# Folding the softmax totals across partitions by adding transfers, so that TensorE sums three tiles instead of eight for the denominators

## The chip, the core and the metric

The kernel runs on one core of a Trainium2 chip. The metric is the device time of one execution in microseconds (us); lower is better. The core has five engines with instruction queues of their own: TensorE (PE in the profile, with its weight loads as PEld), VectorE (DVE), ScalarE (ACT), GpSimd (POOL) and SyncE (SP). Each works through its queue in order and waits on semaphores for what other engines and transfers (DMAs) produce.

## The reference, cut to what matters

Two layers run one after the other on an image tensor of shape 2 x 256 x 64 x 64. The change lies in the first layer, an attention over all 4096 pixels of an image with 8 heads of 32 channels:

```python
q = proj(Wq, bq) / math.sqrt(hd)
k = proj(Wk, bk)
v = proj(Wv, bv)
attn = jax.nn.softmax(jnp.einsum('bnd,bmd->bnm', q, k), axis=-1)
fuse = jnp.einsum('bnm,bmd->bnd', attn, v)
fuse = fuse.transpose(0, 2, 1).reshape(B, C, H, W)
hybrid = _conv1x1(jnp.concatenate([x, fuse], axis=1), Wf, bf)
return hybrid * m + x * (1.0 - m)
```

The second layer computes a channel gate, an attention in 8 x 8 windows, and two 7 x 7 grouped convolutions that give a sigmoid gate. Everything is float32.

The softmax divides by the sum of the exponentials over the 4096 keys. The kernel multiplies the unnormalised exponentials with v, sums the exponentials beside that, and divides afterwards.

## The kernel before, in words

**Work order.** After the projections, `pipeline` (L523) goes through 1024 slots, a list of (b, c, g, m): image b (2), chunk c of 512 queries (8), group g of four heads (2), block m of 128 keys (32). A chunk is therefore 64 slots. This text numbers the 16 chunks 0 to 15 in order of time, and the slots from the chunk's first one, so that slot 63 is a chunk's last and slots 64 on lie in the next chunk. The order on every engine is the order in which the loop at L1196 issues the instructions (`tc.manual_schedule`): in slot i the scores of slot i+2 (L633, TensorE), their exponentials (L646, ScalarE, into a ring of 8 buffers `e`), the products of slot i with v (L669, TensorE), and the sum of the exponentials of slot i (L675, VectorE).

**The totals.** VectorE adds the tiles `e` (128 keys x 4 heads x 512 queries) into two running totals `sum` and `odd`, one for even and one for odd slots ("two chains"), and at a group's last slot adds the two (L677). What remains is a tile of 128 partitions x 4 heads x 512 queries, whose 128 partitions are still to be summed. The last chunk has only one chain, since the buffer of the second is then taken by the convolution.

**The denominators.** `denominators()` (L690) sums the partitions on TensorE: for each of the 8 heads four matmuls (one for each 128 queries, each into its own 32 output partitions) with the constant weights `keysum`, which hold ones in the column of that head. The 32 matmuls add into one PSUM tile `dn`, of which ScalarE makes the copy `inv` (L702); VectorE takes the reciprocal (L721); GpSimd's queue stores it to DRAM (L707, four transfers) and reads it back spread over 32 partitions for each head into `rd` (L714, four transfers); VectorE multiplies the attention result `f` with it (L727).

**Delays written out by hand.** `at(delay, action)` puts an action off by so many slots; `run_later` issues what is due at the end of a slot. The denominators come DN = 8 slots after a chunk's last slot, thus in slot 71; reciprocal, store and spread in slot 72; the multiplication L727 in slot 78. In slot 79 the chunk is handed to `stage` (L731), a generator that does the rest of the chunk in steps; `run_stages` takes a step in every fourth slot, the first in slot 80. The first step multiplies x and f with WfT (`hy`, L519): 32 instructions with x, then 32 with f. The last step adds into `xo` (L974) and stores it to `xs` (L989, GpSimd's queue). For chunk 0, L727 comes 9 slots and the first step 12 slots later.

**Buffers.** Tiles with one `tag` share the buffers of that tag. `psum2` has two PSUM buffers in this phase; `dn` takes one of them between two scores. The totals `sum` have three buffers.

Of the kernel before, what the change touches and what calls it, by code (L numbers as in the profile page):

```python
# [10 lines left out]
F32 = mybir.dt.float32  # L11
I32 = mybir.dt.int32
AF = mybir.ActivationFunctionType
ALU = mybir.AluOpType
# [3 lines left out]
B, C, H, W = 2, 256, 64, 64  # L18
N = H * W
P = 128  # L20
KC = C // P
CH = 512
NCHUNK = N // CH
HEADS0, HD0 = 8, 32
NPAIR = HEADS0 // 2
HG = 4
# [4 lines left out]
EB = 8  # L31
DN = 8
# [16 lines left out]
UW = UG * KS  # L49
# [8 lines left out]
def conv_seq_kernel(ctx: ExitStack, tc: tile.TileContext, a, out):  # L58
    nc = tc.nc
    const = ctx.enter_context(tc.tile_pool(name="const", bufs=1))  # L60
# [12 lines left out]
    def psum2(name):  # L73
        return ps["pair"].tile([P, 2, CH], F32, tag="s", name=name)
# [19 lines left out]
    keysum = const.tile([P, HEADS0, 4, HEADS0], F32, name="keysum")  # L94
    nc.gpsimd.memset(keysum, 0.0)
    for h in range(HEADS0):
        nc.gpsimd.memset(keysum[:, h, :, h : h + 1], 1.0)
    xo = const.tile([P, KC, WS, WP], F32, name="xo")
    nc.gpsimd.memset(xo, 0.0)
    cbias1 = const.tile([P, NU], F32, name="cbias1")  # L100
# [226 lines left out]
    def spread(row, n):  # L327
        f = row.shape[-1]
        return row.rearrange("p u f -> u p f").to_broadcast([NU, n, f])
# [37 lines left out]
    with (  # L367
# [8 lines left out]
        for n in ("WqT", "WkT", "WvT"):  # L376
            t = w0.tile([P, KC, C], F32, name=n)
# [4 lines left out]
        for n in ("bq", "bk"):  # L382

            t = w0.tile([P, KC], F32, name=n)
# [31 lines left out]
        for i, (b, c) in enumerate(chunks):  # L416
            load_chunk()
            x = xs0[i]
            sq = st0.tile([P, 2 * KC, CH], F32, tag="sq", name=f"sq_{b}_{c}")
            tops = st0.tile([P, 2 * KC, CH // 4], F32, tag="top4", name=f"top4_{b}_{c}")  # L420
            for n, w in (("q", wq), ("k", wk)):
                s = psum2(f"{n}0_{b}_{c}")
                for g in range(KC):
                    for kc in range(KC):
                        rhs = x[:, kc, :]
                        if n == "q":
# [5 lines left out]
                            start=(kc == 0),  # L432
                            stop=(kc == KC - 1),
                        )
                t = st0.tile([P, KC, CH], F32, tag=n, name=f"{n}st_{b}_{c}")
# [24 lines left out]
        for i, (b, c) in enumerate(chunks):  # L460
            s = psum2(f"v0_{b}_{c}")
            sv = s.rearrange("p a (t o) -> p (a t) o", t=2)
            for m in range(4):
                for kc in range(KC):
# [4 lines left out]
                        start=(kc == 0),  # L469
                        stop=(kc == KC - 1),  # L470
# [21 lines left out]
            elif i == 2:  # L492
# [3 lines left out]
                for oc in range(KC):  # L496
                    for kc in range(KC):
# [4 lines left out]
                            start=(kc == 0),  # L502
                            stop=(kc == KC - 1),
# [19 lines left out]
    def pipeline(arm, shifted, pools):  # L523
        fp, xpool, gp, wp, avp, ctx_conv = pools
        cpool = ctx_conv.enter_context(tc.tile_pool(name=f"conv{arm}", bufs=1))
# [14 lines left out]
            for g in range(KC)  # L540
            for m in range(NMB)
        ]
        kts, vts, qts, xts, fts, mts = {}, {}, {}, {}, {}, {}
        es, acc, first, totals = {}, {}, {}, {}
        now = [0]
        later = deque()
        stages = deque()

        def at(delay, action):
            later.append((now[0] + delay, action))  # L550
# [13 lines left out]
        def load_q(b, c):  # L564
            q = qp.tile([P, KC, CH], F32, tag="q", name=f"q{arm}_{b}_{c}")
            nc.sync.dma_start(q, q_s[b, c].rearrange("p (g n) -> p g n", g=KC))
            qts[b, c] = q
# [83 lines left out]
            return lambda: exp(*parts[-1])  # L651


        def products(i):
            b, c, g, m = slots[i]
            chains = 1 if (b, c) == (B - 1, NCHUNK - 1) else 2
            if m == 0:
                acc[0] = avp.tile([P, CH], F32, tag="av", name=f"av{arm}_{i}")
                acc[1] = ep.tile([P, HG, CH], F32, tag="sum", name=f"sum{arm}_{i}", bufs=3)
                totals[b, c, g] = acc[1]  # L660
                if chains == 2:
                    room = cpool.tile([P, ROOM], F32, tag="room", name=f"odd{arm}_{i}")
                    acc[2] = room[:, 0 : HG * CH].rearrange("p (h n) -> p h n", h=HG)
            av = acc[0]
            e, v = es[i], vts[b, c, g, m // PB]
            start, stop = m == 0, m == NMB - 1
            for j in range(HG):
                r = slice(32 * j, 32 * j + 32)
                nc.tensor.matmul(av[r, :], v[:, m % PB, r], e[:, j, :], start=start, stop=stop)  # L669
            e = es.pop(i)  # L670
            if m < chains:
                first[m] = e
            else:
                total = acc[1 + m % chains]
                nc.vector.tensor_add(total, first.pop(m % chains, total), e)  # L675
            if stop and chains == 2:
                nc.vector.tensor_add(acc[1], acc[1], acc[2])  # L677
            if stop:
                if g == 0:
                    fts[b, c] = fp.tile([P, KC, CH], F32, tag="f", name=f"f{arm}_{b}_{c}")  # L680
                f = fts[b, c]
                nc.scalar.copy(f[:, g, :], av)
                if g == 0:
                    return
                both = [totals.pop((b, c, gg)) for gg in range(KC)]
                inv = fp.tile([P, P], F32, tag="inv", name=f"inv{arm}_{i}")
                rd = fp.tile([P, KC, 4, P], F32, tag="rd", name=f"rd{arm}_{i}")


                def denominators():  # L690
                    s = psum2(f"dn{arm}_{i}")
                    for h in range(HEADS0):
                        for q in range(4):
                            r = slice(32 * q, 32 * q + 32)
                            nc.tensor.matmul(  # L695
                                s[r, 0, 0:P],
                                keysum[:, h].rearrange("p i h -> p (i h)"),
                                both[h // HG][:, h % HG, q * P : (q + 1) * P],
                                start=(h == 0),
                                stop=(h == HEADS0 - 1),  # L700
                            )
                    nc.scalar.copy(inv, s[:, 0, 0:P])  # L702


                def store_inv(engines):
                    for q in range(4):
                        engines[q % len(engines)].dma_start(  # L707
                            inv_s[b, c][:, :, q].rearrange("h g n -> g h n"),
                            inv[32 * q : 32 * q + HEADS0],
                        )  # L710

                def spread(engines):
                    for h in range(HG):
                        engines[h % len(engines)].dma_start(  # L714
                            rd[32 * h : 32 * h + 32].rearrange("p g q n -> p (g q n)"),
                            inv_s[b, c][h].rearrange("g q n -> (g q n)").partition_broadcast(32),
                        )

                late = EB + 1 if (b, c) == (0, 0) else 0
                at(DN, denominators)  # L720
                at(DN + 1, lambda: nc.vector.reciprocal(inv, inv))  # L721
                queues = (nc.gpsimd,)
                if (b, c) == (B - 1, NCHUNK - 1):
                    queues = (nc.sync, nc.gpsimd)
                at(DN + 1, lambda: store_inv(queues))
                at(DN + 1, lambda: spread(queues))
                at(DN + 7 + late, lambda: nc.vector.tensor_mul(f, f, rd.rearrange("p g q n -> p g (q n)")))  # L727

# [271 lines left out]
        def convolve():  # L1002
# [8 lines left out]
            for k in range(2):  # L1011
                t = cpool.tile([P, B * nb, WP], F32, name=f"yc{arm}{k}")
# [4 lines left out]
            weights = deque([*range(1, NU), 1])  # L1017
            dst = out.rearrange("b (g i) r w -> b i r g w", i=4)

            def load_w(u):  # L1020
                if u >= NU:
                    return
                n = 2 * 32 * UW
                if u == 0:
                    t = cpool.tile([P, n], F32, name=f"w{arm}{u}")
                else:
                    t = ep.tile([P, HG, CH], F32, tag="e", name=f"w{arm}{u}")
                    t = t.rearrange("p h n -> p (h n)")[:, 0:n]
                nc.sync.dma_start(t, w_s[u])
                ws[u] = t  # L1030
# [149 lines left out]
        def run_stages():  # L1180
            while stages:
                waits = next(stages[0], stages)
                if waits is not stages:
                    return waits
                stages.popleft()
# [9 lines left out]
            scores(i)()  # L1195
        for i, (b, c, g, m) in enumerate(slots):  # L1196
            now[0] = i
            if (b, c, g, m) == (B - 1, NCHUNK - 1, 0, 12):
                for _ in banded:
                    pass  # L1200
                conv = convolve()
                next(conv)
            if m % PB == 0:
                load_piece(i // PB + AHEAD)
            if g == KC - 1 and m == 0:
                nxt = (b, c + 1) if c + 1 < NCHUNK else (b + 1, 0)
                if nxt[0] < B:
                    load_q(*nxt)
            rest = scores(i + 2) if i + 2 < len(slots) else None
            products(i)  # L1210
            if rest:
                rest()
            if g == KC - 1 and m == NMB - 1:
                late = EB + 5 if (b, c) == (0, 0) else 0
                at(DN + 8 + late, lambda b=b, c=c: stages.append(stage(b, c)))
            run_later()
            if i % 5 == 1:
                next(banded, None)
            if i % 4 == 0:
                run_stages()  # L1220
# [102 lines left out]
```

## Time and profile before

| | us |
|---|---|
| median of 3 runs | 2924.72 (2922.76 to 2928.86) |
| the profiled execution, its own time | 2921.04 |
| its span in the profile | 2919.3 |
| PE busy | 2881.9 (99%) |
| ACT busy | 2455.9 (84%) |
| DVE busy | 2434.9 (83%) |
| POOL busy | 315.1 (11%) |
| denominators on PE (L695) | 1% of the chain that ended last |
| granted TensorE clock, mean | 0.996 |

The span is the stretch from the first to the last instruction of the profiled execution. "Busy" is the time in which an engine worked on an instruction. Matmuls overlap one another and their ends are modelled, so a busy PE isn't PE at its peak, and the distance between the starts of two groups tells more than their durations. The timeline of an engine gives on each line the start, the duration, the engine, the line of the code, the operation, the tiles written and read, the shapes and how many instructions were merged; in brackets the engine's idle time ahead and what ended it.

### The profile page before, as it was taken

To read this page: it belongs to the slowest core of one execution; us is meant where nothing else is said; L and a number is where in the kernel's file an instruction comes from. 1 tells how busy PE (TensorE), PEld (TensorE's weight loads), DVE (VectorE), ACT (ScalarE), POOL (GpSimd) and SP (SyncE) were. 2 spreads that over 40 slices of the span, in tenths; PEclk is the share of its full clock that TensorE was granted. 3 is DMA by queue.
4 is the path that set the end of the run, shared out by engine and by line. 5 is a ranking of instruction groups with operands and counts; after the bars stand their busy time and mean duration, and the time that the engine had idled before them with its cause. 6 is when DMAs were issued, how large, how long until landed. Compare 5 with 4: busy or idle time off the path is not lost.

```text
span 2919.3 us, 85528 instructions
## 1 busy us (share of the span) xinstructions
PE 2881.9 (99%) x37322; PEld 837.2 (29%) x37322; DVE 2434.9 (83%) x1356; ACT 2455.9 (84%) x4143; POOL 315.1 (11%) x560
## 2 busy tenths in 40 slices
PE   9999999999999999999999999999999999999998
PEld 3551222222222222222222222222222222222665
DVE  3339999899999898998989999989899899999211
ACT  5569989898989898988989898989899898989433
POOL 8010000000000101010000000000101010000356
PEclk9999999999999999999999999999999999999999
DMA  8545422222232323242222223222324232232474
GB/s 245 202 172 174 134 75 63 78 68 80 56 88 65 90 61 91 65 80 71 70 75 69 79 55 82 64 83 63 77 73 84 70 73 75 69 113 88 117 228 120
DMA packets 231124, 276.26 MB, mean 95 GB/s; under 512 B 118672, under 2 KB 135252, under 8 KB 230484
## 3 DMA queue, kind: packets, MB, share of 16 engines
q1 hardware_dynamic: 200996, 231.74, 27.3%
q0 software_dynamic: 22416, 35.61, 5.5%
q8 instruction: 295, 4.83, 0.7%
q10 hardware_dynamic: 7328, 3.36, 0.4%
q14 instruction: 89, 0.73, 0.1%
HBM read 221.88 MB, written 66.39 MB: 99 GB/s over the span
## 4 chain that ended last, share of the span: by engine, by line
PE 97%; DMA 1%; ACT 1%; DVE 0%; issue 0%; SPq 0%; POOL 0%; ACTq 0%; DVEq 0%; POOLq 0%
PE sa L633 37%; PE ava L669 35%; PE hya L519 4%; PE qka L519 4%; PE c2a L1082 2%; PE q L428 2%; PE c1a L1057 2%; PE opa L519 2%; PE vwa L519 2%; PE v L465 2%; PE k L428 2%; PE dna L695 1%; PE sca L847 1%; PE pta L922 1%; PE oa L941 1%; PE ca2a L785 1%
## 5 line engine op out<-in xcount | busy, mean ns | idle before, releaser
L646 ACT ACTIVATE ea<-sa 128x512 f32<-128x512 f32 (+1 forms) x3072 | 2036.7, 746 | 51.6 <-PE sa L633 26.6
L633 PE MATMUL sa<-qa,ka 32*64 32x512 f32 x16384 | 1145.9, 613 | 1.5 <-ACT vst L473 1.2
L675 DVE TENSOR_TENSOR suma<-suma,ea 128x2048 f32<-128x2048 f32 x480 | 1097.4, 2286 | 5.7 <-ACT ea L646 0.5
L669 PE MATMUL ava<-ea,va 128*32 128x512 f32 x8192 | 1091.1, 605 | 1.0
L675 DVE TENSOR_TENSOR odda<-odda,ea 128x2048 f32<-128x2048 f32 x420 | 959.4, 2284 | 50.6 <-ACT ea L646 50.6
L633 PEld LDWEIGHTS sa<-qa,ka 32*64 32x64 f32 x16384 | 241.7, 129 | 785.4 <-ACT ea L646 713.6
L669 PEld LDWEIGHTS ava<-ea,va 128*32 128x32 f32 x8192 | 161.5, 108 | 834.1 <-issue 804.6
L989 POOL DMA_DIRECT2D xs<-xo x94 | 66.6, 716 | 1761.8 <-DVE xo L974 1758.8
L675 DVE TENSOR_TENSOR suma<-ea,ea 128x2048 f32<-128x2048 f32 x32 | 73.2, 2287 | 58.8 <-ACT ea L646 58.8
L519 PE MATMUL qka<-ua,qkv_w 128*32 128x512 f32 x1024 | 115.8, 592 | 0.3 <-DVE ua L803 0.3
L1130 POOL DMA_DIRECT2D out_dram<-za x180 | 101.3, 571 | 77.8 <-DVE za L1110 56.3
L447 DVE TENSOR_REDUCE top<-sq 128x512 f32<-128x2048 f32 x16 | 36.6, 2286 | 81.6 <-ACT sq L441 81.6
L750 ACT ACTIVATE ta<-hya,bf 128x512 f32<-128x512 f32 x32 | 20.2, 683 | 97.3 <-PE hya L519 91.3
L1110 DVE TENSOR_TENSOR za<-za,xla 128x768 f32<-128x768 f32 x24 | 23.0, 960 | 94.3 <-ACT za L1099 53.7
L707 POOL DMA_DIRECT2D invs<-inva x62 | 34.1, 558 | 599.2 <-DVE inva L721 438.9
L754 DVE TENSOR_TENSOR ta<-ta,mca 128x512 f32<-128x512 f32 x32 | 22.0, 688 | 77.4 <-ACT ta L750 77.4
L868 ACT ACTIVATE ewa<-ewa,mxwa 128x64 f32<-128x64 f32 x256 | 85.3, 346 | 1.5 <-DVE mxwa L859 1.5
L1082 PE MATMUL c2a<-yca,wa 32*64 32x192 f32 (+1 forms) x2688 | 83.7, 387 | 2.6 <-issue 2.3
L1093 ACT ACTIVATE za<-c2a 128x384 f32<-128x384 f32 x64 | 27.8, 486 | 57.9 <-PE c2a L1082 41.6
L826 ACT ACTIVATE qka<-qka,qkv_b 128x512 f32<-128x512 f32 x64 | 40.3, 681 | 40.8 <-PE qka L519 40.8
L1082 PEld LDWEIGHTS c2a<-yca,wa 32*64 32x64 f32 x2688 | 64.7, 192 | 22.0 <-issue 12.7
L677 DVE TENSOR_TENSOR suma<-suma,odda 128x2048 f32<-128x2048 f32 x30 | 68.8, 2292 | 1.0
(138 smaller groups left out, 1675.9 us busy)
## 6 DMA issues: line engine op xcount, KB each, us to landing
ka<-ks SPq DMA_DIRECT2D x256, 256.0 KB
va<-vs SPq DMA_DIRECT2D x256, 256.0 KB
wa<-ws SPq DMA_DIRECT2D x17, 896.0 KB
ws<-zeros SPq DMA_DIRECT2D x16, 896.0 KB
xs<-xo POOLq DMA_DIRECT2D x78, 140.0 KB, 6.0
xla<-xs SPq DMA_DIRECT2D x24, 420.0 KB
x<-in_x_dram SPq DMA_DIRECT2D x16, 512.0 KB
qs<-qst SPq DMA_DIRECT2D x16, 512.0 KB
```

What stands on the lines that cost most here:

```text
L428: nc.tensor.matmul(s[:, g, :], w[:, kc, g * P : (g + 1) * P], rhs, start=(kc == 0), stop=(kc == KC - 1),)
L465: nc.tensor.matmul(sv[:, m, :], xs0[i][:, kc, m * P : (m + 1) * P], wv[:, kc, :], start=(kc == 0), stop=(kc == KC - 1),)
L519: nc.tensor.matmul(out[o : o + 32], weights[:, o : o + 32], x, start=start, stop=stop)
L633: nc.tensor.matmul(heads[j][o], k[r, cols][:, o], q[r, g, :], start=True, stop=not shifted)
L646: nc.scalar.activation(e[:, h, :], tile, AF.Exp, scale=SCALE0)
L669: nc.tensor.matmul(av[r, :], v[:, m % PB, r], e[:, j, :], start=start, stop=stop)
L675: nc.vector.tensor_add(total, first.pop(m % chains, total), e)
L677: nc.vector.tensor_add(acc[1], acc[1], acc[2])
L868: nc.scalar.activation(e[:, n, :], e[:, n, :], AF.Exp, bias=mx[:, n : n + 1], accum_out=rs[:, n : n + 1],)
L989: eng.dma_start(x_s[b, n, p + r0 : p + r1].rearrange("r g w -> g r w"), xo[64 * h : 64 * h + 64, oc, r0 - WS * c : r1 - WS * c, :],)
L1082: nc.tensor.matmul(tiles[j // 2][o, j % 2, 0 : n * W], w[r, d, o], y[r, 0:n, d : d + W], start=(d == 0), stop=(d == KS - 1),)
L1130: eng.dma_start(*args)
```

## The change

`fold` is new. When the total of group 0 of a chunk is done (slot 31), 16 transfers on GpSimd's queue lay its four quarters of 32 partitions on top of one another: for each head, the first quarter is copied, and the other three are added by the transfer itself (`accum_op=add`). The four heads come to lie in the four quarters of one tile of 128 partitions x 512. For group 1 (slot 63) it is eight transfers: each head is folded once, to 64 partitions, and two heads share a tile. The results are three tiles of 128 x 512, which lie in one buffer with the tag `w0`; a tile of the convolution's weights, which had a buffer of its own, now shares it. `denominators` has three steps of four matmuls with the new constant weights `foldsum`, instead of eight steps with `keysum`.

The denominators move from slot 71 to slot 73, reciprocal, store and spread from 72 to 74, L727 from 78 to 80 (chunk 0: 87 to 89). The hand-over to `stage` moves from slot 79 to 80, and since L727 stands ahead of it in the list, the first step still falls in slot 80, now right behind L727 (chunk 0: slot 92, as before). The last chunk keeps its old way. In the last chunk the generator of the convolution, with its first loads, is created in slot 16 instead of slot 12.

```diff
@@ constants
+    foldsum = const.tile([P, 3, 4, HEADS0], F32, name="foldsum")
+    nc.gpsimd.memset(foldsum, 0.0)
+    for h in range(HEADS0):
+        n, rows = (0, 32) if h < HG else (1 + (h - HG) // 2, 64)
+        p = rows * (h % HG if h < HG else h % 2)
+        nc.gpsimd.memset(foldsum[p : p + rows, n, :, h : h + 1], 1.0)
+    foldsum = foldsum.rearrange("p n i h -> p n (i h)")
@@ pipeline
+        def fold(total, b, c, g):
+            if g == 0:
+                t = cpool.tile([P, 2 * 32 * UW], F32, tag="w0", name=f"fold{arm}_{b}_{c}")
+                folds[b, c] = [t[:, n * CH : (n + 1) * CH] for n in range(3)]
+            rows = 32 * (g + 1)
+            for k in range(P // rows):
+                for h in range(HG):
+                    dst = folds[b, c][0 if g == 0 else 1 + h // 2]
+                    p = rows * (h if g == 0 else h % 2)
+                    nc.gpsimd.dma_start(
+                        dst[p : p + rows],
+                        total[rows * k : rows * k + rows, h, :],
+                        accum_op=ALU.add if k else ALU.bypass,
+                    )
@@ products
                 nc.scalar.copy(f[:, g, :], av)
+                if chains == 2:
+                    fold(totals.pop((b, c, g)), b, c, g)
                 if g == 0:
                     return
-                both = [totals.pop((b, c, gg)) for gg in range(KC)]
+                both = [] if chains == 2 else [totals.pop((b, c, gg)) for gg in range(KC)]
+                parts = folds.pop((b, c), [])
@@ denominators
-                    for h in range(HEADS0):
+                    terms = [
+                        (keysum[:, h].rearrange("p i h -> p (i h)"), both[h // HG][:, h % HG, :])
+                        for h in range(HEADS0 if both else 0)
+                    ]
+                    terms += [(foldsum[:, n], part) for n, part in enumerate(parts)]
+                    for n, (weights, x) in enumerate(terms):
                         for q in range(4):
                             r = slice(32 * q, 32 * q + 32)
                             nc.tensor.matmul(
                                 s[r, 0, 0:P],
-                                keysum[:, h].rearrange("p i h -> p (i h)"),
-                                both[h // HG][:, h % HG, q * P : (q + 1) * P],
-                                start=(h == 0),
-                                stop=(h == HEADS0 - 1),
+                                weights,
+                                x[:, q * P : (q + 1) * P],
+                                start=(n == 0),
+                                stop=(n == len(terms) - 1),
                             )
@@ delays
-                at(DN, denominators)
-                at(DN + 1, lambda: nc.vector.reciprocal(inv, inv))
+                wait = DN + 2 * (chains == 2)
+                at(wait, denominators)
+                at(wait + 1, lambda: nc.vector.reciprocal(inv, inv))
...
-                at(DN + 1, lambda: store_inv(queues))
-                at(DN + 1, lambda: spread(queues))
-                at(DN + 7 + late, lambda: nc.vector.tensor_mul(f, f, rd.rearrange("p g q n -> p g (q n)")))
+                at(wait + 1, lambda: store_inv(queues))
+                at(wait + 1, lambda: spread(queues))
+                at(wait + 7 + late, lambda: nc.vector.tensor_mul(f, f, rd.rearrange("p g q n -> p g (q n)")))
@@ load_w
-                    t = cpool.tile([P, n], F32, name=f"w{arm}{u}")
+                    t = cpool.tile([P, n], F32, tag="w0", name=f"w{arm}{u}")
@@ loop over slots
-            if (b, c, g, m) == (B - 1, NCHUNK - 1, 0, 12):
+            if (b, c, g, m) == (B - 1, NCHUNK - 1, 0, 16):
...
-                late = EB + 5 if (b, c) == (0, 0) else 0
-                at(DN + 8 + late, lambda b=b, c=c: stages.append(stage(b, c)))
+                late = EB + 4 if (b, c) == (0, 0) else 0
+                at(DN + 8 + ((b, c) != (B - 1, NCHUNK - 1)) + late, lambda b=b, c=c: stages.append(stage(b, c)))
```

## The prediction, made before the changed kernel ran

> **What bounds the kernel now.** I read the busy times first, then the chain that ended last, then the waits, then timelines of chunk 3, which stands for chunks 2 to 13.
>
> ```profile
> PE 2881.9 (99%) x37322; PEld 837.2 (29%) x37322; DVE 2434.9 (83%) x1356; ACT 2455.9 (84%) x4143; POOL 315.1 (11%) x560
> PE 97%; DMA 1%; ACT 1%; DVE 0%; issue 0%; SPq 0%; POOL 0%; ACTq 0%; DVEq 0%; POOLq 0%
> ACT inva L702 <- PE dna L695: 13.4, 16, 1.3
> ```
>
> TensorE is the bound, 97% of the chain, and around the denominators ScalarE waits for it: 13.4 us for all 16. So TensorE time taken out there should leave the span. The timeline of TensorE around them gives the price (start, duration, line):
>
> ```profile
> 810.61 1.07 PE L669 MATMUL ava<-ea,va 128*32 128x512 f32 x8
> 811.61 1.11 PE L633 MATMUL sa<-qa,ka 32*64 32x512 f32 x16
> 812.65 1.07 PE L669 MATMUL ava<-ea,va 128*32 128x512 f32 x8
> 813.53 1.93 PE L695 MATMUL dna<-suma,keysum 128*32 128x128 f32 x64
> 815.39 1.11 PE L633 MATMUL sa<-qa,ka 32*64 32x512 f32 x16
> ...
> 833.64 3.62 PE L519 MATMUL hya<-xa,WfT 128*32 128x512 f32 x32
> 837.08 3.62 PE L519 MATMUL hya<-fa,WfT 128*32 128x512 f32 x32
> ```
>
> A slot lasts 2.04 us (score to score, 809.57 to 811.61). The products take 1.00 us to the next start where scores follow (810.61 to 811.61), but 0.88 where the denominators follow (812.65 to 813.53): the difference, 0.12 us, is the change from arrays of 128*32 to 32*64. The denominators take 815.39 - 813.53 = 1.86 us, less that 0.12 leaves 1.74, or 0.218 us for each of eight heads.
>
> VectorE is next. Its timeline of the same chunk (L677 is slot 63, L721 slot 72, L727 slot 78):
>
> ```profile
> 796.80 2.29 DVE L677 TENSOR_TENSOR suma<-suma,odda 128x2048 f32<-128x2048 f32 x1
> ...
> 816.17 0.95 DVE L721 RECIPROCAL inva<-inva 128x128 f32<-128x128 f32 x1
> ...
> 830.18 1.22 DVE L727 TENSOR_TENSOR fa<-fa,rda 128x1024 f32<-128x1024 f32 x1
> 831.32 2.29 DVE L675 TENSOR_TENSOR odda<-odda,ea 128x2048 f32<-128x2048 f32 x1
> 833.52 2.29 DVE L675 TENSOR_TENSOR suma<-suma,ea 128x2048 f32<-128x2048 f32 x1
> ```
>
> An add takes 2.20 us (831.32 to 833.52), more than a slot. Between stage steps VectorE falls behind, without a gap from slot 66 to slot 80, and catches up while TensorE does `hy` (it then waits 5.70 us for ScalarE, L754). f is ready at 831.40 and wanted at 837.08: 5.68 us to spare.
>
> **The Trainium skill.** "TensorE: Matmul & The Clock Gate", Part 3, says that matmuls start and end strictly in order: a denominator that waits for a transfer holds all scores and products behind it. The trace agrees in chunk 15, where `hy` waits 1.7 us for L727 and nothing overtakes. "TensorEngine Tiling (Array Packing)", Key Properties, says that a change of tiling mode drains the array: here 0.12 us. "DMA: Bandwidth & Descriptors", Rules for kernel authors, says that an adding transfer must wait for the earlier one into the same bytes; that makes the rounds below. Its fit (Anatomy of one DMA), 2.0 us + bytes/436e3, would be 2.15 to 2.3 us for 64 to 128 KB; the trace has 3.2 us for 128 KB, and I use that. None of these prices an adding transfer.
>
> **The change part by part.**
>
> *Matmuls.* Five of eight groups go in 15 chunks: 5 x 0.218 = 1.09 us a chunk, 15 x 1.09 = 16.4 us. The drain stays. ScalarE doesn't take the gain's place: it idles about 0.8 us on each side of L702 there and needs 0.27 us for it. The waits for transfers ahead of these matmuls cost TensorE's sequencer from 0 to 0.2 us a chunk (one such wait on L695 shows 0.05 us, and there may be four); the queue runs ahead, I take 0.
>
> *Transfers.* 24 a chunk, 360 in all, 31 MB, on POOL's queue. An issue takes 0.5 to 0.7 us (L707 0.56, L989 0.72), so about 200 us of an engine that is 11% busy. For an adding transfer the landing is bounded by 1.6 us (the shortest L707) and 10.8 us (the longest L989), since no trace shows one. I take 3.2, the row that moves as much:
>
> ```profile
> rda<-invs POOLq DMA_DIRECT2D x62, 128.0 KB, 3.2
> xs<-xo POOLq DMA_DIRECT2D x78, 140.0 KB, 6.0
> ```
>
> Group 0's four rounds start at slot 31, when POOL has nothing else, and have 40 slots. Group 1 has two rounds: 0.3 us to start, landing of the first round 3.2, 0.2 for the semaphore, three more issues 1.65, landing 3.2: 8.6 us. They start at the end of L677, 799.09. The denominators come at 813.53 + 2 x 2.04 = 817.6, 18.5 us later. Cover: ten slots; it is gone at a landing of 8.2 us. Behind the waiting transfers in POOL's queue stand the eight stores L989 (799.99 before, now about 806, 5.8 us); nobody waits for them before the next chunk. Then come L707 and L714, which would be held only if L989 landed after 822.
>
> *Chunk 0* is tighter: VectorE lags by four slots, L677 ends at 330.80, and slot 73 is 337.39 + 4.08 = 341.5. That is 10.7 us for 8.6, enough up to a landing of 4.2.
>
> *The move by two slots.* L721, L707, L714 and L727 keep their distances of six slots, but two adds now stand ahead of L727: it ends 2 x 2.20 = 4.40 us later, while TensorE is 1.09 us earlier. To spare in chunks 2 to 13: 5.68 - 4.40 - 1.09 = **0.19 us**. The cover of L727 is used up. The spread now matters too: in the trace it landed 0.3 to 3.1 us ahead of L727, and in chunk 6 L727 waited 0.64 us, which would now cost 0.45. Two slots change what the transfers meet, so I take 0.2 us a chunk (0 to 0.6). Chunk 1, where VectorE runs level with TensorE, has 5.08 - 4.40 = 0.7 to spare. Chunk 0: 4.22 - 4.40 - 1.09 = -1.27, so its gain is lost and 0.2 us with it.
>
> *Chunk 14* is different, since the next chunk has one chain of adds, 2.39 us each, and one add more:
>
> ```profile
> 2580.84 1.22 DVE L727 TENSOR_TENSOR fa<-fa,rda 128x1024 f32<-128x1024 f32 x1
> 2583.76 3.62 PE L519 MATMUL hya<-fa,WfT 128*32 128x512 f32 x32
> ```
>
> L727 ends at 2582.06 + 4.77 = 2586.8; TensorE would want it at 2583.76 - 1.09 = 2582.7. It waits 4.1 us, net +3.0. VectorE, which waited 1.5 us at L754 here, now waits about 4.4; it has some 1 us of gaps left in the last chunk, so this isn't won back.
>
> *The rest.* Nine memsets (about 1 us) at the start stand on POOL ahead of loads of small weights, while TensorE projects for 185 us; cost 0, at most 1 if that cover fails. The shared buffer `w0` is wanted by the next fold at slot 95, 22 slots after the denominators; the convolution's loads come four slots later but are used 44 slots on. Both 0, at most 1 us if SP's queue waited for the buffer with key loads behind it.
>
> Sum: chunks 1 to 13, 13 x (-1.09 + 0.2) = -11.6; chunk 0 +0.2; chunk 14 +3.0: **-8.4 us**. The profiled execution's own time is 2921.04 (span 2919.3 and 1.7 around it): 2912.6. It stands 3.7 below the median of the runs, 2924.72: **2916** there.
>
> **The rivals.**
>
> *The spread or VectorE eats the gain (no change).* Every delay of f over 0.19 us is paid by TensorE at once. For: landings of L714 vary from 2.5 to 6.0 us, and POOL and the transfers get more to do. Against: the folds are over before L707. If f came 0.9 us late on average in 13 chunks, -14.2 + 11.7 + 3.2 = +0.7: 2925.
>
> *The folds become the bound (slower).* The place: the first matmul of the denominators, slot 73. The price: what two rounds take above 18.5 us, so it begins at a landing of 8.2 us and passes the gain at 8.8. For: an adding transfer must read its destination too, and L989, strided, reaches 10.8. Against: rows of 2 KB, 64 to 128 KB. At 9 us, two rounds take 20.2: 1.7 late, net 0.6 x 13 = 8; chunk 0 late by 9.5, net 8.4; chunk 14 3: +19, 2944. At 10 us about 2970.
>
> *The heads are not independent.* If each transfer waited for the one before, group 1 would need 8 x 3.4 = 27 us, 8.7 late: 13 x 7.6 and some 20 in chunks 0 and 14, about 2920 + 119 = 3043. Against: the four L714, into four quarters of `rd`, are issued 0.5 us apart.
>
> **How the numbers follow.** A measurement can tell about 0.2%, 5.8 us, from no change. Forecast 0.62, from 2909 (no late f, none in chunk 14 either) to 2921 (0.6 us in each chunk); of it 0.55 lie below 2918.9 and 0.07 within. Gain eaten, 0.16: 0.14 within, 0.02 slower. Late folds 0.18 and serial folds 0.04, slower. Faster 0.55, same 0.21, slower 0.24. The range goes from 2909 to 2940, which leaves out the serial folds and most late folds.
>
> **What would show it.** Right: L695 with 24 instructions in 0.77 us to the next score, no wait on it; L727 directly ahead of `hy` with f, TensorE waiting under 0.5 us for it in most chunks and about 4 in chunk 14; chunks of 157.7 to 158 us instead of 158.8. Wrong: a wait of L695 for a transfer (landings over 8 us), or a wait of `hy` for L727 of a microsecond in every chunk.

## The result and the profile after

| | before | after |
|---|---|---|
| median of 14 runs each, in turn on one chip, us | 2925.09 (2921.39 to 2930.67) | 2925.60 (2919.37 to 2929.27) |
| profiled execution, own time (span), us | 2921.04 (2919.3) | 2927.96 (2926.2) |
| start of the last convolutions (first matmul L1088, before L1057), us | 2700.25 | 2696.27 |
| from there to the end of the span, us | 219.01 | 229.91 |

The ratio is 0.9998 [0.9991, 1.0005]: no change, against a forecast of 8.4 us less. The two profiled executions make it look like a loss, since that of before lies 4.1 us under its median and that of after 2.4 us over its own. The two last rows show the pattern all the same: a gain up to the end of the slots, and a larger loss in the 8% of the span that follow, where the change touches almost nothing. (I call these two stretches **the slots** and **the rest**.)

The page of after, busy times and chain:

```profile
PE 2873.4 (98%) x36722; PEld 821.6 (28%) x36722; DVE 2437.0 (83%) x1356; ACT 2455.0 (84%) x4143; POOL 568.6 (19%) x929
PE 91%; DMA 3%; DVE 2%; issue 2%; ACT 1%; POOL 1%; SPq 0%; ACTq 0%; DVEq 0%; POOLq 0%
```

TensorE has 600 matmuls and 8.5 us of work less (the trace counts two for each of these matmuls of the code, of which 300 are gone), yet its share of the chain fell from 97% to 91%: it now waits. For what, its table of waits says (total, times, longest, us; "issue" is time in which it waited for nothing that the profile shows):

```profile
PE hya L526 <- DVE fa L758: 9.1, 5, 4.0
PE c1a L1088 <- ACT yca L1096: 6.3, 2, 5.7
PE c1a L1088 <- issue: 5.9, 2, 4.5
...
PE dna L725 <- DMA folda<-suma: 3.0, 2, 1.9
```

Before, `hy` waited once for f, 1.7 us; "issue" ahead of the convolutions cost 2.3 us, on L1082. L526, L725, L758 are the former L519, L695, L727.

**The gain is there.** TensorE's timeline in chunk 3:

```profile
817.29 0.84 PE L725 MATMUL dna<-folda,foldsum 128*32 128x128 f32 x24
818.06 1.16 PE L640 MATMUL sa<-qa,ka 32*64 32x512 f32 x16
...
832.27 3.62 PE L526 MATMUL hya<-xa,WfT 128*32 128x512 f32 x32
836.80 3.64 PE L526 MATMUL hya<-fa,WfT 128*32 128x512 f32 x32 [0.91 <-DVE fa L758]
```

The denominators take 818.06 - 817.29 = 0.77 us instead of 1.86, in each of chunks 1 to 14 and without a wait. But f comes late here: `hy` with f starts 4.53 us after `hy` with x, where it took 3.44 before: 1.09 us, the whole gain of this chunk. The chain of waits in this stretch shows who made f late (start, duration, what):

```profile
799.05 3.55 DMA folda<-suma
...
805.35 1.64 POOL folda L670 x2
806.99 0.65 POOL xs L1020
...
807.87 8.83 DMA xs<-xo
...
823.14 6.19 DMA invs<-inva
...
831.39 4.00 DMA rda<-invs
...
835.52 1.24 DVE fa L758
```

The folds hold GpSimd's queue until 807. So the eight stores to `xs` (L1020, before L989) are issued from 806.4 to 814.9, instead of 800.0 to 806.8, and the last lands at 827.4. The inverse's stores were issued at 821.5 to 823.7, into that traffic, and the last takes 6.19 us. The spread can't be issued before 829.9 and lands at 835.4; VectorE is ready 1.2 us earlier. The page prices the transfers (busy us, mean ns of one issue; then KB and median us to landing):

```profile
L670 POOL DMA_DIRECT2D folda<-suma x360 | 252.7, 899 | 1787.7 <-DVE suma L699 1043.2
...
folda<-suma POOLq DMA_DIRECT2D x240, 64.0 KB, 3.1
folda<-suma POOLq DMA_DIRECT2D x120, 128.0 KB, 3.9
...
xs<-xo POOLq DMA_DIRECT2D x78, 140.0 KB, 7.9
```

In the slots of the profile of after, the last `xs` store landed after the inverse's first store was issued in chunks 3, 6 and 12 (by 5.9, 1.1 and 0.7 us), and in no other from 2 to 14, as far as landings are recorded. These are the three whose f was late by the spread: 1.09, 1.15 and 0.69 us. In the other ten of chunks 1 to 13, f was ready 0.22 us (chunk 1: 0.53) ahead of `hy`. The stores to `xs` aren't the whole reason, though. In a second profile of after, chunks 4, 5 and 13 also had such a landing, by 1.0 to 1.9 us, without a late f. And in the kernel before, these same three chunks have the longest time from the inverse's first store to the first issue of the spread: 6.1, 5.9 and 6.5 us in its second profile, against 4.7 to 5.0 in the other nine of chunks 2 to 13 (in its first, 5.1 to 5.5 against 4.6 to 5.2). There f has about 5 us or more to spare, so it costs nothing. What makes these three slow wasn't tested.

**Chunk 0** waits for its folds:

```profile
340.75 0.40 PE L725 MATMUL dna<-folda,foldsum 128*32 128x128 f32 x8
342.28 0.43 PE L725 MATMUL dna<-folda,foldsum 128*32 128x128 f32 x8 [1.13 <-DMA folda<-suma]
344.62 0.43 PE L725 MATMUL dna<-folda,foldsum 128*32 128x128 f32 x8 [1.91 <-DMA folda<-suma]
344.97 1.11 PE L640 MATMUL sa<-qa,ka 32*64 32x512 f32 x16
```

4.22 us to the next score instead of 0.77. The first transfer of group 1's first round was issued at 330.38 and landed at 337.03; the second round landed at 344.48.

**Chunk 14** waits for VectorE, and then runs at half clock:

```profile
2570.40 3.62 PE L526 MATMUL hya<-xa,WfT 128*32 128x512 f32 x32
2578.07 5.34 PE L526 MATMUL hya<-fa,WfT 128*32 128x512 f32 x32 [4.05 <-DVE fa L758]
2583.33 1.11 PE L640 MATMUL sa<-qa,ka 32*64 32x512 f32 x16
```

The second line should last 3.62 us. The table by stretches, whose column behind the five busy times (PE, PEld, DVE, ACT, POOL) is PEclk, the granted clock, says why:

```profile
2578.10:2579.10 1.00, 1.00 (x12) 0.38 (x16) 0.00 (x0) 0.00 (x0) 0.00 (x0) 0.99 0.00 0
2579.10:2582.50 3.40, 3.40 (x24) 0.85 (x16) 0.00 (x0) 0.00 (x0) 0.00 (x0) 0.50 0.02 5
2582.50:2585.90 3.40, 3.40 (x48) 0.62 (x40) 1.62 (x3) 2.43 (x4) 0.00 (x0) 1.00 0.00 0
```

The wait cost 4.23 us, the half clock 1.7 more.

**The rest.** It is 10.90 us longer, and four places make up about that much. L526 waits for f of chunk 15 2.63 us instead of 1.68 (+0.97 between its two halves), and the half clock after that wait makes it 5.34 us long (+1.72). The stretch from the 13th to the 15th group of c1a takes 19.10 us instead of 12.43 (+6.67). And the span goes on for 15.89 us behind TensorE's last matmul, instead of 14.25 (+1.64). The wait ahead of the ninth group of c1a is longer too, 5.73 us instead of 4.09, but adds nothing: counted from the start of the rest, the group comes 2.57 us later, no more than the wait for f and its half clock. TensorE's timeline, chunk 15 and then the stretch:

```profile
2709.05 3.63 PE L526 MATMUL hya<-xa,WfT 128*32 128x512 f32 x32
2715.30 5.34 PE L526 MATMUL hya<-fa,WfT 128*32 128x512 f32 x32 [2.63 <-DVE fa L758]
...
2801.52 2.20 PE L1088 MATMUL c1a<-xla,wa 128*32 128x192 f32 x47
2805.10 0.70 PE L1088 MATMUL c1a<-xla,wa 128*32 128x192 f32 x9 [1.37 <-issue]
2805.73 2.64 PE L1113 MATMUL c2a<-yca,wa 32*64 32x192 f32 x112
2808.30 0.56 PE L1088 MATMUL c1a<-xla,wa 128*32 128x192 f32 x6
2813.34 4.64 PE L1088 MATMUL c1a<-xla,wa 128*32 128x192 f32 x50 [4.49 <-issue]
```

Before, the same groups go through:

```profile
2802.48 2.54 PE L1057 MATMUL c1a<-xla,wa 128*32 128x192 f32 x56
2804.95 2.64 PE L1082 MATMUL c2a<-yca,wa 32*64 32x192 f32 x112
2807.52 2.54 PE L1057 MATMUL c1a<-xla,wa 128*32 128x192 f32 x56
```

In after, TensorE stands still in the middle of a group, without a semaphore to wait for. The two places are 127 matmuls with their weight loads apart, 254 instructions. The group behind the longer standstill takes 4.64 us at half clock instead of some 2.3.

So the questions were: is the loss in the rest the change's doing or chance; what are chunks 0, 3, 6, 12 and 14 worth; and what is the standstill?

### The profile page after: what moved, and what is told of

Same layout as the page of the kernel before. It is cut to its first block, busy times and chain, and to the rows that moved or that the text cites. A ratio compares the mean times of both kernels' runs of the same rounds, so it can differ in the third digit from the quotient of the medians.

```text
span 2926.2 us, 84951 instructions
## 1 busy us (share of the span) xinstructions
PE 2873.4 (98%) x36722; PEld 821.6 (28%) x36722; DVE 2437.0 (83%) x1356; ACT 2455.0 (84%) x4143; POOL 568.6 (19%) x929
## 4 chain that ended last, share of the span: by engine, by line
PE 91%; DMA 3%; DVE 2%; issue 2%; ACT 1%; POOL 1%; SPq 0%; ACTq 0%; DVEq 0%; POOLq 0%
PE sa L640 34%; PE ava L691 33%; PE qka L526 4%; PE hya L526 3%; PE c1a L1088 2%; PE c2a L1113 2%; PE vwa L526 2%; PE opa L526 2%; PE v L472 2%; PE q L435 2%; PE k L435 1%; DVE suma L697 1%; DMA invs<-inva 1%; PE sca L878 1%; PE oa L972 1%
## 5 line engine op out<-in xcount | busy, mean ns | idle before, releaser
L670 POOL DMA_DIRECT2D folda<-suma x360 | 252.7, 899 | 1787.7 <-DVE suma L699 1043.2
L526 PE MATMUL qka<-ua,qkv_w 128*32 128x512 f32 x1024 | 116.2, 592 | 0.3 <-DVE ua L834 0.3
L1088 PE MATMUL c1a<-xla,wa 128*32 128x192 f32 (+1 forms) x896 | 64.1, 435 | 11.6 <-issue 5.9
L1020 POOL DMA_DIRECT2D xs<-xo x94 | 72.0, 1017 | 11.0 <-DVE xo L1005 8.3
```

The source lines that it names most:

```text
L526: nc.tensor.matmul(out[o : o + 32], weights[:, o : o + 32], x, start=start, stop=stop)
L670: nc.gpsimd.dma_start(dst[p : p + rows], total[rows * k : rows * k + rows, h, :], accum_op=ALU.add if k else ALU.bypass,)
L1020: eng.dma_start(x_s[b, n, p + r0 : p + r1].rearrange("r g w -> g r w"), xo[64 * h : 64 * h + 64, oc, r0 - WS * c : r1 - WS * c, :],)
L1088: nc.tensor.matmul(s[32 * j : 32 * j + 32, 0 : n * W], w[:, j, d, :], xs[k][:, 0:n, j, d : d + W], start=(d == 0), stop=(d == KS - 1),)
```

## The experiments

All ratios are to the kernel before, run in turn with each on one chip; below 1 is faster.

**Both kernels again, unchanged.**

> The kernel before, unchanged, for a second profile. In the first one the slots ended (start of the first convolution group) at 2700.3 us and the rest took 219.0. Theory 'ends': the saving on TensorE is real and is given back in the slots of chunks 0, 1 and 14; what the convolution at the end takes differs from run to run with either kernel. Then the slots end again at 2700 to 2701 and the rest takes anything from 219 to 230. Rival 'tail': the change makes the convolution slower, and it takes 219 again here.

> The changed kernel, unchanged, for a second profile. In the first one the slots ended at 2696.3 us and the rest took 229.9. Both theories: slots end at 2696 to 2697. 'Ends': the rest takes between 219 and 230, no longer on average than in the kernel before, and the ratio is 0.998 to 1.000. 'Tail': about 230 again.

Measured: before 2929.16 us, 1.0004 [0.9993, 1.0015]; after 2929.02, 1.0001 [0.9992, 1.001]. The slots ended at 2700.91 and 2700.64, the rest took 221.73 and 228.81. No change, once more. The slots of after missed their 2696 to 2697: the wait in chunk 0 was only 0.6 us longer (3.62 us of idle time instead of 3.04), but this time the clock fell. TensorE's timeline there:

```profile
345.80 0.66 PE L725 MATMUL dna<-folda,foldsum 128*32 128x128 f32 x8 [2.10 <-DMA folda<-suma]
346.38 2.01 PE L640 MATMUL sa<-qa,ka 32*64 32x512 f32 x16
348.32 1.94 PE L691 MATMUL ava<-ea,va 128*32 128x512 f32 x8
350.19 1.69 PE L640 MATMUL sa<-qa,ka 32*64 32x512 f32 x16
351.81 1.07 PE L691 MATMUL ava<-ea,va 128*32 128x512 f32 x8
```

Scores of 1.11 us take 2.01; 6.8 us at half clock. The longer rest is no chance: its standstills came at the same two matmuls as in after, 1.37 and 2.56 us.

**The delays alone.** Before, with the new delays and hand-over, but no fold, the old matmuls and w0's own buffer.

```diff
-                at(DN, denominators)
-                at(DN + 1, lambda: nc.vector.reciprocal(inv, inv))
+                wait = DN + 2 * (chains == 2)
+                at(wait, denominators)
+                at(wait + 1, lambda: nc.vector.reciprocal(inv, inv))
...
-                at(DN + 7 + late, lambda: nc.vector.tensor_mul(f, f, rd.rearrange("p g q n -> p g (q n)")))
+                at(wait + 7 + late, lambda: nc.vector.tensor_mul(f, f, rd.rearrange("p g q n -> p g (q n)")))
```

> The kernel before with the later slots alone (denominators in 73, reciprocal and spread in 74, multiplication of f in 80, hand-over in 80, chunk 0 likewise), no transfers and all eight heads summed by TensorE. 'Ends': nothing is gained, f has 5.68 - 4.40 = 1.3 us to spare in chunks 1 to 13, and comes 4.77 - 1.71 = 3.1 us late in chunk 14, where TensorE's clock may halve for another 1.7: slots end at 2703 to 2705, ratio 1.001 to 1.002. Rival 'the later slots cost nothing': slots end at 2700, ratio 1.000.

Measured: 2929.98 us, 1.0006 [0.9997, 1.0014]; slots 2703.12, rest 218.73. In chunks 2 to 13 f was 1.27 us early, so 5.68 - 4.40 holds. Chunk 14 in TensorE's timeline:

```profile
2580.03 3.62 PE L519 MATMUL hya<-xa,WfT 128*32 128x512 f32 x32
2586.61 3.64 PE L519 MATMUL hya<-fa,WfT 128*32 128x512 f32 x32 [2.96 <-DVE fa L728]
```

It waits 3.0 us, here without a fall of the clock. The wait of chunk 14 is thus made by the delays, and the delays do not lengthen the rest.

**Chunk 14 the old way; chunks 0 and 14 the old way.** No fold, eight matmul steps and old delays there:

```diff
+            folding = chains == 2 and (b, c) not in ((B - 1, NCHUNK - 2),)
...
-                if chains == 2:
+                if folding:
...
-                both = [] if chains == 2 else [totals.pop((b, c, gg)) for gg in range(KC)]
+                both = [] if folding else [totals.pop((b, c, gg)) for gg in range(KC)]
...
-                wait = DN + 2 * (chains == 2)
+                wait = DN + 2 * folding
```

(For the second, the tuple also has `(0, 0)`.)

> The changed kernel, but chunk 14 keeps the old way: no fold, eight heads, denominators in slot 71, f multiplied in slot 78. 'Ends': the wait of 4.2 us in front of its last matmuls goes, and with it 3.4 us at half clock, against 1.1 us for the five heads: slots end 4.8 us earlier, at 2691.5, ratio 0.9975 to 0.9985. 'Tail': the slots end as early, but the convolution still takes 230, ratio 0.999 to 1.000.

> The changed kernel with chunks 0 and 14 in the old way (no fold, eight heads, slot 71), chunks 1 to 13 as changed. 'Ends': besides what the run with chunk 14 alone in the old way gained, the wait of 3.7 us of chunk 0's denominators for their transfers goes, and the half clock of 6.8 us after it; slots end 3.3 us earlier than there, at about 2694, ratio 0.996 to 0.9972. Rival: chunk 0's wait is only VectorE's lag, which comes back at f: slots end at 2697 as there, ratio 0.9976.

Measured: 2921.89 us, 0.9976 [0.9969, 0.9983], and 2917.16, 0.9972 [0.9962, 0.9982]. With chunk 14 the old way, `hy` follows there after 3.44 us, without a wait. But in this profile the slots ended at 2697.54, not at the 2691.5 expected: chunk 0 brought the half clock, chunks 6 and 12 waited 2.7 and 1.9 us for f, and TensorE stood still for 1.4 us in chunk 3. With chunk 0 the old way too, its `hy` with f starts at 383.90 instead of 387.05, and the slots end at 2690.29, ten us ahead of before. In after the slots gained 4 us and in its repetition nothing, so the two ends ate six to ten of these ten. Chunks 3, 6 and 12 still waited in this profile, 1.5, 1.8 and 1.7 us. The rest was 224.79 and 223.35 long, less than in after, and 40 or 80 more matmuls stand ahead of it. Whether that is the reason is the next question but one.

**One slot earlier; no adding rounds.**

```diff
-                wait = DN + 2 * (chains == 2)
+                wait = DN + 1 * (chains == 2)
```

> The changed kernel with the denominators and all that follows them one slot earlier (72, 73, f in 79; hand-over unchanged). If the last place before the matmuls is what f loses by: 2.4 us to spare in chunks 1 to 13 instead of 0.2, no wait in chunks 3, 6 and 12, chunk 14 waits 1.8 us instead of 4.2 and without half clock; the folds still land in time except in chunk 0, whose denominators wait 2 us longer. Slots end at 2690 to 2693, ratio 0.997 to 0.999. If the folds are too late for slot 72 (landed up to 15 us after the last add, slot 72 comes 16.5 after), L725 waits in chunks beyond 0 and the ratio is 1.000 or above.

```diff
-            for k in range(P // rows):
+            for k in range(1):
```

> The changed kernel without the adding transfers: only the first quarter (half) of each total is copied, so the denominators are sums over part of the keys. Matmuls, slots and buffers as changed. It shows what the adding rounds cost. If they are what delays f in chunks 3, 6 and 12 (their issue pushes the eight stores to x_s into the store of the inverses) and the denominators of chunk 0: those waits go, 1.1 + 1.2 + 0.7 and 3.4 us; slots end at 2688 to 2693, chunk 14 still waits 4.2. If the adding transfers cost nothing: slots end at 2696 to 2700 as in the changed kernel.

Measured: one slot earlier 2923.89 us, 0.9992 [0.9986, 0.9999], a smaller gain than the 0.997 to 0.999 expected; no adding rounds 2919.70, 0.9981 [0.9974, 0.9988]. One slot earlier left f 2.42 us early and no wait in chunks 3, 6 and 12; in chunk 14 `hy` still waited 3.1 us, not the 1.8 expected, since there the spread landed late (2574.2), and the clock fell behind this wait and in chunk 0. In the second, POOL's timeline of chunk 3 is as short as in before:

```profile
797.18 2.05 POOL L670 DMA_DIRECT2D folda<-suma  x4 [74.84 <-DVE suma L699]
801.90 5.58 POOL L1020 DMA_DIRECT2D xs<-xo  x8 [2.67 <-issue]
819.63 2.21 POOL L737 DMA_DIRECT2D invs<-inva  x4 [12.15 <-DVE inva L752]
826.61 2.01 POOL L744 DMA_DIRECT2D rda<-invs  x4 [4.77 <-DMA invs<-inva]
```

The spread is issued 7.0 us after the inverse, not 8.4, and chunks 3, 6 and 12 together wait 0.2 us for f instead of 2.9. Chunk 0 no longer waits for its folds; instead `hy` waits there 1.26 us for f, the 1.27 that the prediction works out. So the adding rounds, 240 of the 360 transfers, are what makes these four chunks late. That they do it in chunks 3, 6 and 12 by pushing the stores to `xs` into the inverse's isn't shown: without them the spread is issued 1.4, 1.5 and 0.1 us sooner after the inverse there, but still 7.0 to 7.6 us, against 4.4 to 6.0 in the other nine of chunks 2 to 13.

**Where the instruction stream is cut.** "Runtime: NRT & Kernel Launch", Instruction fetch mechanics, in the Trainium skill says that an engine fetches its instructions in blocks of 16 KiB, 256 of them, and that crossing a boundary is mostly hidden. The traces agree on the size (the instruction queue's packets are 16384 bytes; the standstills are 127 or 128 pairs apart), but not that it is hidden. The change takes 600 pairs away, so the boundaries fall on other matmuls of the rest. To test it, tiny matmuls into an unused PSUM tile were put ahead of everything, inside the 5.8 us in which TensorE waits for its first weights: 30 in after, to move its boundaries off these places, and 34 in before, to bring boundaries to the places of after. The trace counts two pairs for each.

```diff
+        pad = psum1("pad")
+        for _ in range(30):
+            nc.tensor.matmul(pad[0:32, 0:1], ones[:, 0:32], ones[:, 0:1], start=True, stop=True)
```

> The changed kernel with 30 tiny matmuls (32 columns by 1) ahead of the first projection, where TensorE waits 5.8 us for weights; their sum isn't used. They move the rest of TensorE's instruction stream by some 60 pairs of weight load and matmul. In both profiles of the changed kernel TensorE stands still in the convolution at the same two instructions (1.37 us, then 4.49 and 2.56 us) 127 pairs apart and with no semaphore to wait for. Theory 'fetch': these are places where the instructions themselves arrive late, beside the large loads of convolution weights; moved by 60 pairs they fall elsewhere, the stretch from the 13th to the 15th convolution group takes 12.5 to 13.5 us as in the kernel before, not 15.8 to 19.1, ratio 0.998 to 0.9995. Rival: it waits for data there; nothing moves, 15.8 to 19.1 us, ratio 1.000.

> The kernel before with 34 tiny matmuls ahead of the first projection, within TensorE's wait there, which bring its fetch boundaries to the convolution instructions at which the changed kernel stands still. 'Fetch': the kernel before, with nothing else changed, gets the standstills of the 13th and 14th group (1.4 us, then 2.5 to 4.5 us, perhaps with half clock); that stretch takes 16 to 19 us instead of 12.4 to 13.3, ratio 1.001 to 1.002. Rival: the standstills belong to the change; the stretch stays at 12.4 to 13.3, ratio 1.000.

Measured: after with 30, 2922.19 us, 0.9987 [0.998, 0.9994], rest 220.34; before with 34, 2928.25, 1.0001 [0.9993, 1.0009], rest 220.98. In the first, TensorE goes through both places:

```profile
2796.00 2.54 PE L1091 MATMUL c1a<-xla,wa 128*32 128x192 f32 x56 [0.17 <-DMA xla<-xs]
2798.47 2.79 PE L1116 MATMUL c2a<-yca,wa 32*64 32x192 f32 x112
2801.19 2.54 PE L1091 MATMUL c1a<-xla,wa 128*32 128x192 f32 x56
```

The stretch from the 13th to the 15th group takes 13.49 us, as in before (12.43, 13.32). Its standstills now lie where before has them: at the 1120th, 1630th and 2651st matmul of the rest, for 1.0, 0.8 and 1.5 us, in before 0.6, 1.7 and 0.6. In before with 34, standstills moved to the places foreseen, but were short:

```profile
2803.71 0.82 PE L1060 MATMUL c1a<-xla,wa 128*32 128x192 f32 x10 [0.61 <-issue]
...
2808.93 2.51 PE L1060 MATMUL c1a<-xla,wa 128*32 128x192 f32 x50 [1.35 <-issue]
```

14.42 us, not 16 to 19, and no slower. Counted from the start of the queue they stand at matmuls 35308 and 35436, where unpadded before, in its second profile, has 35309 and 35436, while the work at these numbers moved by 68. So the place of a standstill goes with the number of instructions ahead: shown. Its length isn't explained by the place alone. With after's boundaries it was 4.5, 2.6, 3.9 and 2.8 us at the longer one in four profiles (after twice, no adding rounds, one slot earlier), and 1.35 in before with 34. The load of the DMA engines does not order them: they were 68% busy in the longest, 81 to 96% in the three others and 51% in the shortest. What decides the length stays open. The size of the gain is to be read from the ratios: about 0.12% less than after, some 3 to 4 us. How much of it comes from the standstills isn't shown: in this profile chunk 0 waited 1.2 us for its folds instead of 3.0 and f of chunk 15 kept `hy` waiting 1.58 us without half clock, two things that the test wasn't to touch. The profiled run of the shifted kernel was the shortest of its 19, 6.9 us under their median.

**Together.** Chunks 0 and 14 the old way, the others one slot earlier (`wait = DN + 1 * folding`); and the same with 55 tiny matmuls.

> Chunks 0 and 14 in the old way, and in chunks 1 to 13 the denominators in slot 72 and f in slot 79. The two gains should add: slots ended at 2690.3 with the ends in the old way, and there chunks 3, 6 and 12 still waited 1.5, 1.8 and 1.7 us for f, which is 2.2 us earlier now. Slots end at 2685 to 2686, ratio 0.995 to 0.9965. If instead the inverses arrive no earlier because of the stores to x_s, as in chunk 14 of the run with slot 72, the waits stay: 2690, ratio 0.9972.

> The same with 55 tiny matmuls ahead of the first projection, so that TensorE's fetch boundaries fall at the same convolution instructions as in the kernel before. They take about 1.7 us more than the wait there. 'Fetch': the standstills of 2.4, 1.3 and 1.1 us seen with the ends in the old way go, the stretch from the first convolution group to the end takes 219 to 221 us instead of 223 to 225; net 1 to 3 us better than without. Rival 'no fetch': 1.7 us worse.

Measured, beside 2929.36 us for before: 2918.62, 0.9959 [0.9947, 0.9971], and 2915.50, 0.9953 [0.9942, 0.9965]. Both beat before, by some 11 and 14 us, and after too by their ratios. That the 55 tiny matmuls add to the gain isn't shown: the intervals overlap, and the rest took 221.75 us with them, not the 219 to 221 expected, and 221.71 without, not the 223 to 225. The slots of the first missed their 2685 to 2686 (2697.35): in its profile the spreads of chunks 3 and 6 landed at 834.4 and 1313.5, TensorE waited 2.9 and 4.1 us and the clock fell twice. One of the two in TensorE's timeline:

```profile
829.45 3.62 PE L526 MATMUL hya<-xa,WfT 128*32 128x512 f32 x32
835.82 5.34 PE L526 MATMUL hya<-fa,WfT 128*32 128x512 f32 x32 [2.75 <-DVE fa L759]
```

One slot earlier also moves the inverse's stores closer behind the stores to `xs`, and it isn't a sure cure for these chunks: the second version waited 1.1, 2.7 and 1.1 us in 3, 6 and 12.

## Why the prediction was partly right

It forecast -8.4 us on the profiled execution; the pair of profiles has +6.9, the medians +0.5. Its range held the result, its likeliest case did not: what came is "no change", the outcome of the rival in which late work eats the gain. That rival's 2925 lies on the result by luck: it has f 0.9 us late on average in chunks 1 to 13, where 0.23 was measured, and the largest loss came in the rest, which the forecast and all rivals put at nothing. Step by step:

- **Matmuls, -1.09 a chunk: right.** 1.86 to 0.77 us. The chunks are 157.74 us long instead of 158.79, within the 157.7 to 158 foreseen.
- **The spare time of f, 0.19 us: right.** 0.22 us. The 0.2 us a chunk for late spreads: 2.93 us in 13 chunks is 0.23. From `hy` of chunk 0 to that of chunk 13 the trace gains 10.5 us, foreseen were 11.6. But the mean hides where it fell: the whole loss lies in chunks 3, 6 and 12, where the inverse's stores landed late. The prediction named the limit itself: L707 and L714 would be held only if the stores of L989 landed after 822. In chunk 3 they landed at 827.4. How far these stores are the reason is open.
- **Folds, 8.6 us: too small, cover right.** Two rounds took 10 to 15 us in chunks 1 to 14, which 18.5 us still covered. The step that failed is the landing of 3.2 us in chunk 0, where 4.2 was the limit: 6.6, so 3.45 us of waiting. Chunk 0 cost 1.6 us instead of 0.2, and with the half clock 5.4 (`hy` with f at 390.81 in the second profile of after). The bounds of 1.6 to 10.8 held it; the sum didn't use them for this chunk. Why the landing is so long there wasn't tested.
- **Chunk 14, a wait of 4.1: right (4.2), but +4.9 and not +3.0** for the time up to the end of the slots. The missing term is the clock. The prediction gave no wait of TensorE a price beyond its own length.
- **The stretch behind the slots, which has no term in the sum: wrong, and the largest error.** The prediction's own "rest" is the memsets and the shared buffer, and looks no further. Measured were +10.9 us in this pair, +7.1 in the other. Of the first, 6.7 lie at the two standstills and the half clock they brought, 2.7 at f of chunk 15 with its half clock, 1.6 behind the last matmul; in the other pair it was 2.5, 3.4 and 2.0. Taking 600 matmuls out moves every later block boundary; no step looked at that. The delays are excluded (rest 218.73), and so are the shared buffer and the later loads of the last chunk by themselves, which the run with 30 tiny matmuls keeps (rest 220.34). Why f of chunk 15 and the last stores came later was not tested.

In sum: -8.4, +1.4 for chunk 0, +1.1 for chunks 1 to 13, +1.9 for chunk 14 and +10.9 for the rest make the +6.9. Of the two other rivals, serial folds are refuted, and folds as the bound came true in chunk 0 alone. One sum of the prediction doesn't come out: for serial folds it has "2920 + 119 = 3043", and from 2924.72 it is 3044.

## What to carry to other kernels

Where TensorE is the bound and never stops, a wait put in its way can cost more than its length: count the half clock that may follow it (here 1.7 us for each period of 3.4 us), and look first at chunks whose schedule differs (the first, the last but one). Transfers that are themselves in time can still delay what stands behind them in their queue, as the stores to `xs` here by 6 to 8 us in chunk 3, and make a later transfer late for which someone does wait. And a change that takes instructions out moves the block boundaries of everything after it, so compare late stages too, and try a few idle instructions up front before putting a small loss there down to the work itself.

## What the hardware showed beyond expectation

**The clock falls on a fixed grid.** The half-clock stretches of after, up to the end of the convolutions, begin at 2579.08, 2715.61, 2777.05 and 2811.19 us: 40, 18 and 10 times 3.413 us apart, and all last one or two such periods. Cutting the 13 profiles (before, after and eleven experiments) into this grid and adding up TensorE's idle time in each period gives a rule for these runs (the first 10 us and the end of the program, from 2895 us on, are left out). From full clock, the next period was at half in all 27 cases with 2.05 us or more, in 3 of 10 between 1.73 and 2.05, and in none below. "TensorE: Matmul & The Clock Gate", Part 1, in the Trainium skill has the free-running window of 3.4 us, and the traces agree; it has the clock fall after a window of idleness, and here 60% of one was enough. That explains why 2.63 us cost 1.7 more in chunk 15 of after, while in chunk 0 a wait of 3.45 us, cut by eight matmuls and by the grid into at most 1.8 us a period, left the clock full.
